# Masked attention on one core: context products in groups of four slot blocks, twelve exponentials' buffers, a new deal of the other work

## The chip, the cores and the metric

The kernel runs on one core of one Trainium2 chip. The metric is the time of one execution in device microseconds (us), lower is better. Before the change it is 1081.12 us, the median of three runs (1079.87 to 1084.78).

The engines of the core are named as in the profile: PE is TensorE (matrix products), with PEld for its weight loads, DVE is VectorE, ACT is ScalarE, POOL is GpSimd, and SP is SyncE, which here only issues DMA transfers.

## What is computed

Sixteen batches of self-attention over 1024 tokens with 512 features and 8 heads of 64, in which queries, keys and values are one and the same projection, and a mask of zeros and ones (about half of them ones) says which tokens take part:

```python
xt = jnp.transpose(x, (0, 2, 1))              # x: (16, 512, 1024)
q = xt @ Wq.T
qh = q.reshape(B, T, NH, dk).transpose(0, 2, 1, 3)
scores = scale * jnp.einsum('bhqd,bhkd->bhqk', qh, qh)
logits = (scores * cmask + (1.0 - cmask) * NEG) * rmask
attn = jax.nn.softmax(logits, axis=-1)
ctx = jnp.einsum('bhqk,bhkd->bhqd', attn, qh)
out = ctx.transpose(0, 2, 1, 3).reshape(B, T, D) @ Wo.T
x = x + jnp.transpose(out, (0, 2, 1))
```

A column outside the mask gets no weight. A row outside the mask has equal logits, so its result is the same for all such tokens of a batch: the mean of the values, projected.

## The kernel before

**Slots.** The kernel computes the full attention only for the tokens inside the mask. Their indices are found on the chip (`slots`, `hot`, `index`), their rows are gathered by indirect DMAs on POOL's queue (`gather`, L339) and lie in 544 slots: four blocks of 128 and a tail of 32. Results are scattered back by POOL (L811).

**Matmul precision.** Products of 32-bit numbers are made of 16-bit halves: `xt` transposes the rows (L424), ACT and DVE split them into a high and a low half (L384, L385); a query product (`query`, L447) is twelve matmuls for 128 features and half of the slots. ACT copies it from PSUM (L450) and DVE sets the slots beyond the batch's count to zero (L453). `qsplit` splits the query (L461 to L463), and four DMAs of SP's queue spread the halves over the partitions into the tile `xx` (L468 to L471). One `xx` serves one pair of heads.

**Scores and exponentials.** `scores(b, p, i)` makes the scores of one head p, one block i of 128 slots against all 544, with four matmuls (L620) into one of two PSUM tiles `pss`; ACT takes the exponential (L624) into an SBUF tile tagged `p`, of which there are nine. The tail slots of four heads go together: sixteen matmuls with 32 weight columns (L595), an exponential (L599), two DVE operations (L604, L605), and four DMAs (L611, L612) into `pt`.

**Context.** `attend(b, p, i, ps)` multiplies the values by the exponentials: for a pair of heads and a block, four matmuls of 64 weight columns with 32-bit numbers (L643), each two rows in the trace, adding to one PSUM tile `pav` (there is only one). The trace calls their tile 128\*64; the tile of scores, queries and projections is 128\*128, and that of the tail scores 128\*32. With i = 4 the tail is added (L647) and ACT copies the sum (L651). `recip_sums` (L666 to L674) and `recip_rows` (L680, L683, and DMAs L685, L688 into `rb`) give the rows' reciprocal sums, `norm` (L711 to L717) scales the context by them, and `project` (L727, twelve matmuls of 512 columns, then L732) makes the output.

**Values and peaks.** `value(b, e)` transposes `xx` by matmuls with a constant (L497), ACT copies the values (L500), and DVE sums their squares (L484, L485). From these come, for four heads at once, upper bounds that are subtracted before the exponential: `peaks` (L541, L543), `top` (a transpose on PE, L549, and a reduction on DVE, L551) and `bottom` (a matmul, L558, and small DVE operations from L560 on). `range_x` (L392) is a check of ranges on DVE.

**The order of the work.** `run` loops over the batches. A batch has 18 stages: for each of four pairs of heads the four blocks, and two stages of tail scores (after the second stage, and before the last pair). A stage of a block issues the scores of the pair's first head, then part of a work list `m`, then the scores of the second head, then, in some stages, a group of context products, and then another part of `m`. The list `m` holds what belongs to the batches around: the end of the batch before (reciprocals, `norm`, `project`), and for the next batch the transposes, queries, values and peaks. How much of `m` each stage issues is set by two numbers a stage in `share`.

Context products wait one stage or more: `todo` takes what a stage makes, a stage of block 0 or 2 hands it to `ready`, and a stage of block 1 or 3 issues `ready`, the last block first. So a group holds two blocks, and it comes two stages after the scores of its first block. All matmuls of a group after the first are tied to the first one (`behind`, with high priority), so that a group is not cut. Above this order stands a scheduler that fixes each engine's final order from the issue order, priorities and its own costs; `high_priority` raises what it surrounds. Each engine then takes its instructions in that order and waits at semaphores. The functions `later` and `issue` put the SP and POOL transfers into their queues one by one, stage by stage.

Of the kernel before, what the change touches and what calls it, by code (L numbers as in the profile page):

```python
# [10 lines left out]
F32 = mybir.dt.float32  # L11
# [8 lines left out]
P = 128  # L20
# [10 lines left out]
C = 544  # L31
# [18 lines left out]
class Fast:  # L50
# [531 lines left out]
    def scores(self, b, p, i):  # L582


        nc, s = self.nc, self.st[b]
        if "z" not in s:
            s["z"] = self.sb([P, H, 4], F32, "z", 2)
            s["zt"] = self.sb([P, 2], F32, "zt", 2)
        if i is None:
            pt = self.ps_s.tile([P, 2, 512], F32, tag="s", name="pss")  # L590
            for a in range(2):
                for g in range(2):
                    for r in range(HG):
                        xx, k = s["xx"][2 * p + r // 2], r % 2
                        self.beat = nc.tensor.matmul(pt[r * CT:(r + 1) * CT, g, :CH], lhsT=xx[:, 2 * k, 512:C],  # L595
                                                     rhs=xx[:, 2 * k + a, g * CH:(g + 1) * CH],
                                                     start=(a == 0), stop=(a == 1)).ins
            t = self.sb([P, C], F32, "p", 9)
            nc.scalar.activation(t.rearrange("p (g c) -> p g c", g=2), pt[:, :, :CH], AF.Exp,  # L599
                                 bias=s["nm"][p][:, HG:], scale=SCALE, accum_out=s["zt"][:, p:p + 1])  # L600

            hi = self.sb([P, C], F32R, "c", 4)
            lo = t.bitcast(F32R)
            nc.vector.tensor_copy(hi, t)  # L604
            nc.vector.tensor_tensor(lo, t, hi.bitcast(F32), ALU.subtract)  # L605

            def spread():
                s["pt"] = self.sb([P, 2, C], F32R, "pt")
                half = slice(0, DK), slice(DK, P)
                for k in range(2):  # L610
                    nc.sync.dma_start(out=s["pt"][half[k], k, :].bitcast(F32), in_=hi[half[k]].bitcast(F32))  # L611
                    nc.sync.dma_start(out=s["pt"][half[1 - k], k, :].bitcast(F32), in_=lo[half[k]].bitcast(F32))  # L612

            self.later(spread)
            return None
        xx, k = s["xx"][p // 2], p % 2
        pt = self.ps_s.tile([P, 2, 512], F32, tag="s", name="pss")
        for a in range(2):
            for g in range(2):
                self.beat = nc.tensor.matmul(pt[:, g, :CH], lhsT=xx[:, 2 * k, i * P:(i + 1) * P],  # L620
                                             rhs=xx[:, 2 * k + a, g * CH:(g + 1) * CH],
                                             start=(a == 0), stop=(a == 1)).ins
        t = self.sb([P, C], F32, "p", 9)
        self.exp = [nc.scalar.activation(t.rearrange("p (g c) -> p g c", g=2), pt[:, :, :CH], AF.Exp,  # L624
                                         bias=s["nm"][p // HG][:, p % HG:p % HG + 1], scale=SCALE,
                                         accum_out=s["z"][:, p, i:i + 1]).ins]
        return t

    def attend(self, b, p, i, ps):
        nc, s = self.nc, self.st[b]  # L630

        if i == 1:
            s["pav"] = self.ps_av.tile([P, 2, 512], F32, tag="av", name="pav")
        for g in range(2):
            for k in (1, 0) if i < 4 else range(2):
                cols = slice(g * CH, (g + 1) * CH)
                if i < 4:
                    with ExitStack() as st:
                        if self.group_first:

                            st.enter_context(self.behind(self.group_first))
                            st.enter_context(self.tc.high_priority(offset=HPO))
                        mm = nc.tensor.matmul(s["pav"][k * DK:(k + 1) * DK, g, :CH], lhsT=s["v"][p][:, i, k * DK:(k + 1) * DK],  # L643
                                              rhs=ps[k][:, cols], start=(i == 1), stop=False)
                    self.group_first = self.group_first or mm.ins
                else:
                    nc.tensor.matmul(s["pav"][:, g, :CH], lhsT=s["vt"][p // 2][:, k, p % 2 * 2:p % 2 * 2 + 2, :],  # L647
                                     rhs=s["pt"][:, p % 2, cols], start=False, stop=(k == 1))
        if i == 4:
            c = self.sb([P, C], F32, "c", 4)  # L650
            nc.scalar.copy(c.rearrange("p (g c) -> p g c", g=2), s["pav"][:, :, :CH])  # L651
            s["c"].append(c)
# [192 lines left out]
    def run(self, flag):  # L845
# [14 lines left out]
        def value(n, e):  # L860
            return [(0.45, L(self.value, n, e))]
# [83 lines left out]
        if True:  # L945
            for b in range(B + 1):
                o, n = b - 1, b + 1
                if b == B:
                    self.last(o, todo)
                    break  # L950
                free, sums, rows, third, tail, rest = {}, [], [], [], [], []
                if b:
# [12 lines left out]
                if n < B:  # L965
                    q, x, v = (lambda e, g: query(n, e, g)), xt(n)[2 if b == 0 else 0:], (lambda e: [(0.25, L(self.value, n, e))])
                    tc, tv = ((lambda g, f=f, c=c: [(c, L(f, n, g))]) for f, c in ((self.tail_copy, 0), (self.value_tail, 0.25)))
                    rng = [(0, L(self.range_x, n, c)) for c in range(DC)]
                    ahead = b + 2 < B
                    hot, index = ([(c, L(f, b + 2))] if ahead else [] for f, c in ((self.hot, 0), (self.index, 0.2)))  # L970
                    take = [(0, L(self.gather, b + 2, j)) for j in range(5)] if ahead else []
                    m = sums + x[:2] + (value(b, 3) if b else []) + pk(b, 1) + second + x[2:4] + rows + x[4:]
                    for g in new[0]:
                        m += [(0, L(self.active, *g))]
                    m += q(0, 0) + tp(b, 1) + (q(0, 1) if b else bt(b, 1) + q(0, 1))
                    for g in new[0]:
                        m += [(0.3, L(self.slots, *g))]
                    for g in new[1]:
                        m += [(0, L(self.facts_sums, *g))]
                    m += (bt(b, 1) if b else hot) + q(1, 0) + third + ([] if b else index) + q(1, 1) + ([] if b else take)  # L980
                    for g in new[1]:
                        m += [(0.1, L(self.facts_end, *g))]
                    m += rng[:2] + tc(0) + tail + v(0) + P_(0) + tv(0) + rest + v(1) + P_(1) + (hot if b else []) + rng[2:] + q(2, 0) + (index if b else [])
                    m += pk(n, 0) + q(2, 1) + tp(n, 0) + P_(2) + (take if b else []) + q(3, 0) + v(2) + bt(n, 0)
                    m += q(3, 1) + tc(1) + [(0, L(self.means, n))] + P_(3) + tv(1)
                    if b == 0:
                        k = next(k for k, (c, f) in enumerate(m) if f is index[0][1])
                        for c in range(DC):
                            m.insert(k + 1 + 3 * c, (0, L(self.split, "o", c)))
                else:  # L990

                    places = [("xi", 8), ("xa", 13)]
                    come = [[L(self.late, x, j, *places[k % 2]) for j in range(5, 9)] for k, x in enumerate(rests[b])]
                    leave = [[L(self.rest, x, j) for j in range(5, 9)] for x in rests[b]]
                    free[0] = [L(self.late, b, 4)] + come[0]
                    for c, l in zip(come[1:] + [[]], leave):
                        free[0] += c + l
                    m = second + sums + value(b, 3) + pk(b, 1) + rows + [(0.6, lambda: None)]
                    m += tp(b, 1) + [(0.6, lambda: None)] + bt(b, 1) + [(2.6, L(self.project_means, b))] + third + [(1.2, lambda: None)] + P_(0, 1, 2, 3)
# [13 lines left out]
                    for k in range(2 * DC):  # L1013
                        free.setdefault(1 + k // 3, []).append(L(self.sum_half, 1, k))

                share = [(1.2, 0) if i is None else ((0.95, 0.95), (0.9, 0), (0.45, 0.95), (0.9, 0))[i] for _, i in S]
                unit = sum(c for c, _ in m) / sum(map(sum, share))
                done, goal, pos = 0.0, 0.0, 0

# [8 lines left out]
                for st, (p, i) in enumerate(S):  # L1028
# [13 lines left out]
                    for _ in range(1 if b < B - 2 else -(-len(self.urgent + self.spare) // (N - st))):  # L1042
                        self.issue()

                    if i in (0, 2):
                        ready, todo = todo, []
                    elif i in (1, 3):
                        self.group_first = None
                        for f in ready[1::-1] + ready[2:]:
                            f()  # L1050
                        ready = []
                    fill(share[st][1])
# [157 lines left out]
```

## Time and profile before

| | |
|---|---|
| median of 3 runs | 1081.12 us |
| the profiled execution | 1081.4 us |
| its span, first to last instruction | 1079.7 us |
| mean granted clock of TensorE | 0.995 |
| PE busy | 1038.1 us, 96% of the span |
| DVE busy | 745.6 us, 69% |
| ACT busy | 681.6 us, 63% |
| POOL busy | 303.0 us, 28% |
| mean DMA rate | 168 GB/s |

The profile is one execution, recorded by the hardware. A group line names the source line (L624 is line 624 of the kernel), the engine, the operation, what it writes and reads with the shapes and types, and how often it ran; then the total busy time in us, the mean duration of one in ns, and the idle time of the engine just before such instructions, with what ended it. A line of the waits names the engine and the instruction that waited, what it waited for, and the total in us, the times, and the longest in us. A line of the timeline starts with the time in us from the start of the span and a duration in us; a bracket at its end gives the idle time before it and what ended it. TensorE's instructions overlap and their ends are modelled, so for it the distance from start to start is what tells the time taken. The granted clock is the share of TensorE's full clock that it was given.

### The profile page before, as it was taken

What the parts mean: (1) busy time and instruction counts of PE and PEld (TensorE: products, weight loads), DVE (VectorE), ACT (ScalarE), POOL (GpSimd) and SP (SyncE); (2) the same over time, 40 slices, a digit from 0 to 9 for tenths busy, and PEclk for the clock granted to TensorE, in tenths of its full rate; (3) what the DMA queues carried; (4) which work ended last, traced back from release to release, by engine and by line L of the source; (5) the groups of instructions that cost most, each with busy time, mean ns of one, the idle gap of its engine ahead of it and who ended that gap; (6) DMA issues with size and microseconds to landing.
All of it is one profiled execution on the core that took longest, in us unless ns stands there. A gap on an engine that the chain in (4) does not pass through costs nothing.

```text
span 1079.7 us, 23837 instructions
## 1 busy us (share of the span) xinstructions
PE 1038.1 (96%) x8626; PEld 690.9 (64%) x8626; DVE 745.6 (69%) x2376; ACT 681.6 (63%) x1722; POOL 303.0 (28%) x303
## 2 busy tenths in 40 slices
PE   6889999999999999999999999999999999999996
PEld 6566667666666666666666666667666665666553
DVE  6687768676675767766785776868667775666553
ACT  5777667666676766666576666666666565665550
POOL 3101022222202223222233323222232331335652
PEclk9999999999999999999999999999999999999999
DMA  6746465556655554656556566554755554565752
GB/s 205 211 126 177 133 175 154 174 150 190 174 141 158 171 173 145 198 176 169 177 147 197 154 186 193 152 171 135 229 176 173 177 149 127 149 182 166 222 175 84
DMA packets 78125, 181.39 MB, mean 168 GB/s; under 512 B 15008, under 2 KB 16800, under 8 KB 78000
## 3 DMA queue, kind: packets, MB, share of 16 engines
q1 hardware_dynamic: 56816, 111.62, 36.6%
q0 software_dynamic: 21184, 68.18, 20.8%
q8 instruction: 70, 1.15, 0.5%
q14 instruction: 55, 0.45, 0.1%
HBM read 92.34 MB, written 33.91 MB: 117 GB/s over the span
## 4 chain that ended last, share of the span: by engine, by line
PE 82%; DMA 7%; DVE 3%; ACT 2%; issue 2%; SPq 2%; POOL 0%; POOLq 0%; ACTq 0%; DVEq 0%
PE pav L643 21%; PE pss L620 19%; PE pm L727 15%; PE pm L447 14%; DMA xx<-hl 6%; PE pm L424 3%; PE pav L647 3%; PE pss L595 2%; PE pm L497 2%; PE pm L680 1%; ACT q L450 1%; SPq L470 1%; ACT p L624 1%; PE pm L520 1%; DMA rb<-rd 1%
## 5 line engine op out<-in xcount | busy, mean ns | idle before, releaser
L624 ACT ACTIVATE p<-pss,nm 128x544 f32<-128x544 f32 x512 | 365.5, 717 | 210.5 <-PE pss L620 203.6
L620 PE MATMUL pss<-xx 128*128 128x272 f16 x2048 | 317.6, 280 | 3.1 <-ACT p L624 2.7
L643 PE MATMUL pav<-p,v 128*64 128x272 f32 x2048 | 262.9, 399 | 0.0
L620 PEld LDWEIGHTS <-xx 128*128 128x128 f16 x2048 | 191.9, 100 | 73.2 <-issue 27.7
L643 PEld LDWEIGHTS pav<-p,v 128*64 128x64 f32 x2048 | 135.6, 136 | 94.3 <-issue 27.1
L811 POOL DMA_INDIRECT y_out<-xa,idx x68 | 70.2, 1032 | 288.6 <-issue 91.5
L447 PE MATMUL pm<-xh,wqh 128*128 128x274 f16 (+1 forms) x512 | 143.3, 280 | 3.3 <-DVE nm L560 1.9
L447 PE MATMUL pm<-xl,wqh 128*128 128x274 f16 (+1 forms) x512 | 142.9, 279 | 0.2 <-DVE xl L385 0.2
L447 PE MATMUL pm<-xh,wql 128*128 128x274 f16 (+1 forms) x512 | 143.0, 279 | 0.0
L339 POOL DMA_INDIRECT xa<-x_in,idx x68 | 69.5, 1023 | 167.1 <-PE pss L620 71.0
L447 PEld LDWEIGHTS <-wqh 128*128 128x128 f16 x1024 | 99.3, 98 | 25.9 <-issue 6.7
L811 POOL DMA_INDIRECT y_out<-xi,idx x60 | 74.0, 1233 | 137.7 <-DVE xi L798 38.3
L624 ACT ACTIVATION_READ_ACCUMULATOR p<-pss,nm 128x1 f32 x512 | 102.6, 200 | 0.0
L450 ACT ACTIVATE q<-pm 128x272 f32<-128x272 f32 (+1 forms) x128 | 50.8, 397 | 81.6 <-PE pm L447 81.6
L727 PE MATMUL pm<-woh,ch 128*128 128x512 f16 x240 | 91.8, 382 | 0.3 <-DVE tmp L523 0.3
L727 PE MATMUL pm<-wol,ch 128*128 128x512 f16 x240 | 91.7, 382 | 0.0
L727 PE MATMUL pm<-woh,cl 128*128 128x512 f16 x240 | 91.5, 381 | 0.0
L732 DVE SCALAR_TENSOR_TENSOR xa<-pm,xa 128x512 f32<-128x512 f32 x60 | 41.4, 690 | 72.4 <-PE pm L727 72.3
L339 POOL DMA_INDIRECT xi<-x_in,idx x60 | 61.3, 1021 | 106.1 <-PE pss L620 49.5
L727 PEld LDWEIGHTS <-ch 128*128 128x128 f16 x480 | 46.7, 98 | 45.6 <-issue 2.2
L369 ACT ACTIVATE xm<-xm 128x1024 f32<-128x1024 f32 (+1 forms) x62 | 62.5, 1009 | 2.3 <-DMA xm<-x_nat_in 2.3
L711 DVE TENSOR_TENSOR c<-c,rb 128x544 f32<-128x544 f32 x64 | 46.1, 720 | 22.4 <-PE pss L620 11.1
(194 smaller groups left out, 1550.0 us busy)
## 6 DMA issues: line engine op xcount, KB each, us to landing
xx<-hl SPq DMA_DIRECT2D x256, 136.0 KB
xm<-x_nat_in SPq DMA_DIRECT2D x56, 512.0 KB
rb<-rd SPq DMA_DIRECT2D x128, 136.0 KB
pt<-c SPq DMA_DIRECT2D x64, 136.0 KB
pt<-p SPq DMA_DIRECT2D x64, 136.0 KB
ub<-ud SPq DMA_DIRECT2D x16, 256.0 KB
xi<-x_nat_in SPq DMA_DIRECT2D x8, 256.0 KB
xa<-x_in,idx POOLq DMA_INDIRECT x68, 4.5
```

The costliest lines, as they stand in the source:

```text
L339: dma = self.nc.gpsimd.indirect_dma_start(out=tile[:n], out_offset=None, in_=self.x, in_offset=bass.IndirectOffsetOnAxis(ap=idx, axis=0))
L369: self.nc.scalar.activation(s["xm"][k], s["xm"][k], AF.Copy, accum_out=s["ms2"][:, k:k + 1])
L424: self.pe = nc.tensor.transpose(pt[:, c, :], x[:n, c * P:(c + 1) * P], self.ident[:n, :n]).ins
L447: self.beat = nc.tensor.matmul(pq, lhsT=w[:, c, e * P:(e + 1) * P], rhs=xx[:, c, cols], start=(k == 0), stop=(k == 3 * DC - 1)).ins
L450: nc.scalar.activation(s["q"][:, e, cols], pq, AF.Copy, scale=1.0 / (SX * SW))
L620: self.beat = nc.tensor.matmul(pt[:, g, :CH], lhsT=xx[:, 2 * k, i * P:(i + 1) * P], rhs=xx[:, 2 * k + a, g * CH:(g + 1) * CH], start=(a == ...
L624: self.exp = [nc.scalar.activation(t.rearrange("p (g c) -> p g c", g=2), pt[:, :, :CH], AF.Exp, bias=s["nm"][p // HG][:, p % HG:p % HG + 1 ...
L643: mm = nc.tensor.matmul(s["pav"][k * DK:(k + 1) * DK, g, :CH], lhsT=s["v"][p][:, i, k * DK:(k + 1) * DK], rhs=ps[k][:, cols], start=(i == ...
L711: self.once(nc.vector.tensor_tensor(c, c, s["rb"][p], ALU.mult), self.beat if p < 3 else None)
L727: nc.tensor.matmul(po[:cols.stop - cols.start], lhsT=a[:, e, cols], rhs=w[:, e, :], start=(e == 0 and k == 0), stop=(e == DC - 1 and k == 2))
L732: self.nc.vector.scalar_tensor_tensor(x, po, 1.0 / (SX * SW), x, ALU.mult, ALU.add)
L811: dma = self.nc.gpsimd.indirect_dma_start(out=self.out, out_offset=bass.IndirectOffsetOnAxis(ap=idx, axis=0), in_=x, in_offset=None)
```

## The change

Four things are edited.

- The tiles tagged `p`, which hold the exponentials until they are multiplied, become twelve instead of nine (L598 and L623).
- A group of context products holds the four blocks of a pair of heads. `ready` is taken over in the stage of block 0 only and issued in the stage of block 1 only, that is, in the second stage of the next pair, in the order 3, 2, 1, 0 and then the tail; the start flag of the accumulation moves from block 1 to block 3. `last` issues the blocks of the last pair in the same order.
- The work list `m` is put in another order. Value 3 of the batch goes after four transposes instead of two. The peaks of the batch's second four heads go to the end of the transposes, and their top goes behind the second query product. The values 0, 1 and 2 of the next batch move down: value 0 behind the first projection, value 1 behind the query product (2, 0), value 2 behind (3, 1); the peaks and the top of the first four heads go down with them.
- The numbers in `share` are new: more of `m` is issued in stages of block 2 and less in stages of block 1.

```diff
-            t = self.sb([P, C], F32, "p", 9)
+            t = self.sb([P, C], F32, "p", 12)
...
-        t = self.sb([P, C], F32, "p", 9)
+        t = self.sb([P, C], F32, "p", 12)
...
-        if i == 1:
+        if i == 3:
             s["pav"] = self.ps_av.tile([P, 2, 512], F32, tag="av", name="pav")
...
-                                              rhs=ps[k][:, cols], start=(i == 1), stop=False)
+                                              rhs=ps[k][:, cols], start=(i == 3), stop=False)
...
-                    self.last(o, todo)
+                    self.last(o, todo[3::-1] + todo[4:])
...
-                    m = sums + x[:2] + (value(b, 3) if b else []) + pk(b, 1) + second + x[2:4] + rows + x[4:]
+                    m = sums + x[:2] + second + x[2:4] + (value(b, 3) if b else []) + rows + x[4:] + pk(b, 1)
                     for g in new[0]:
                         m += [(0, L(self.active, *g))]
-                    m += q(0, 0) + tp(b, 1) + (q(0, 1) if b else bt(b, 1) + q(0, 1))
+                    m += q(0, 0) + (q(0, 1) + tp(b, 1) if b else tp(b, 1) + bt(b, 1) + q(0, 1))
...
-                    m += rng[:2] + tc(0) + tail + v(0) + P_(0) + tv(0) + rest + v(1) + P_(1) + (hot if b else []) + rng[2:] + q(2, 0) + (index if b else [])
-                    m += pk(n, 0) + q(2, 1) + tp(n, 0) + P_(2) + (take if b else []) + q(3, 0) + v(2) + bt(n, 0)
-                    m += q(3, 1) + tc(1) + [(0, L(self.means, n))] + P_(3) + tv(1)
+                    m += rng[:2] + tc(0) + tail + P_(0) + v(0) + tv(0) + rest + P_(1) + (hot if b else []) + rng[2:] + q(2, 0) + v(1) + (index if b else [])
+                    m += q(2, 1) + pk(n, 0) + P_(2) + (take if b else []) + tp(n, 0) + q(3, 0) + bt(n, 0)
+                    m += q(3, 1) + v(2) + tc(1) + [(0, L(self.means, n))] + P_(3) + tv(1)
...
-                share = [(1.2, 0) if i is None else ((0.95, 0.95), (0.9, 0), (0.45, 0.95), (0.9, 0))[i] for _, i in S]
+                share = [(1.2, 0) if i is None else ((1.0, 0.6), (0.1, 0.5), (0.9, 1.0), (0.9, 0.9))[i] for _, i in S]
...
-                    if i in (0, 2):
+                    if i == 0:
                         ready, todo = todo, []
-                    elif i in (1, 3):
+                    elif i == 1:
                         self.group_first = None
-                        for f in ready[1::-1] + ready[2:]:
+                        for f in ready[3::-1] + ready[4:]:
                             f()
                         ready = []
```

In the list, `q(e, g)` is a query product, `v(e)` a value of the next batch, `P_(i)` the projection of block i of the batch before, `x` the transposes of the next batch, `pk`, `tp` and `bt` the peaks, top and bottom, `tc` and `tv` the tail's copy and values, `rng` the checks of ranges, and `rows`, `sums`, `second` the reciprocals and the `norm` of the batch before.

## Prediction

> **What bounds the kernel now.** I read the page's busy shares first, then its groups, then TensorE's waits, then the timeline around single places.
>
> ```profile
> PE 1038.1 (96%) x8626; PEld 690.9 (64%) x8626; DVE 745.6 (69%) x2376; ACT 681.6 (63%) x1722; POOL 303.0 (28%) x303
> L624 ACT ACTIVATE p<-pss,nm 128x544 f32<-128x544 f32 x512 | 365.5, 717 | 210.5 <-PE pss L620 203.6
> ```
>
> TensorE is the bound: 1038.1 of 1079.7 us. ScalarE idles 203.6 us before its exponentials because TensorE has not written the scores, so anything gained must come off TensorE's stream: an instruction, a pause between instructions, or a wait. No matmul is removed. TensorE's waits:
>
> ```profile
> PE pm L497 <- DMA xx<-hl: 11.4, 15, 1.9
> PE pss L620 <- ACT p L624: 2.7, 4, 1.1
> PE pm L447 <- DVE nm L560: 1.9, 2, 1.4
> ```
>
> The value transposes (L497) wait 15 times, about once a batch, for the spread of the query they read. Hardly anything else waits. The pauses are seen only in TensorE's timeline; each row gives the start, the modelled duration and the count, so I subtract starts from starts. A stage with a context group, and one at the end where two groups have run together:
>
> ```profile
> 507.64 0.63 PE L620 MATMUL pss<-xx 128*128 128x272 f16 x4
> 508.20 2.06 PE L643 MATMUL pav<-p,v 128*64 128x272 f32 x16
> 510.18 0.33 PE L680 MATMUL pm<-ident,rcol 128*128 128x128 f32 x1
> ...
> 1050.88 1.09 PE L620 MATMUL pss<-xx 128*128 128x272 f16 x8
> 1051.81 0.18 PE L408 MATMUL pm<-okr,on 128*128 128x24 f16 x1
> 1051.91 2.97 PE L643 MATMUL pav<-p,v 128*64 128x272 f32 x24
> 1054.81 0.64 PE L620 MATMUL pss<-xx 128*128 128x272 f16 x4
> ```
>
> **Part 1: groups of four blocks.** Eight L620 take 1051.81 − 1050.88 = 0.93 us, so four take 0.46; before the group four take 508.20 − 507.64 = 0.56. Entering costs 0.10. Sixteen rows take 510.18 − 508.20 = 1.98, twenty-four 1054.81 − 1051.91 = 2.90: eight rows cost 0.92, so sixteen would cost 1.84, and 0.14 is paid once however long the group is. A group therefore costs 0.24 us beyond its matmuls. The order of the built kernel has 64 groups of 32 rows for 128 of 16. 64 × 0.24 = **−15.4 us**. The Trainium skill gives a reason and another price: "TensorEngine Tiling (Array Packing)", Key Properties, says that changing the tiling mode drains TensorE (L643 is 128*64, its neighbours 128*128), and "TensorE: Matmul & The Clock Gate", Single matmul latency, puts a drain at some 175 ns; two drains a group would be an estimated 350 ns, 64 × 0.35 = 22 us. I take the row.
>
> What the group needs hides it: its first block is now the one whose exponential came last, but the scheduler puts at least 1.6 us of other TensorE work between that score and the group. The twelve p buffers (nine before) hold eight waiting tiles, the tail tile and the next three; the order places the group ahead of the score that would need a thirteenth. Without that cover each group would wait one exponential, 0.72 us.
>
> **Part 2: tail scores in one piece.** The order shows L595 in 35 pieces instead of 62. In 14 batches the tail stage of heads 0 to 3 was cut as in the last six lines; the first two are an uncut one, of heads 4 to 7:
>
> ```profile
> 532.09 0.65 PE L595 MATMUL pss<-xx 128*32 128x272 f16 x16
> 532.67 0.64 PE L620 MATMUL pss<-xx 128*128 128x272 f16 x4
> ...
> 554.12 0.29 PE L595 MATMUL pss<-xx 128*32 128x272 f16 x1
> 554.34 0.33 PE L680 MATMUL pm<-ident,rcol 128*128 128x128 f32 x1
> 554.60 0.53 PE L595 MATMUL pss<-xx 128*32 128x272 f16 x12
> 555.06 0.43 PE L424 MATMUL pm<-ident,xt 32*128 32x32 f32 x4
> 555.42 0.30 PE L595 MATMUL pss<-xx 128*32 128x272 f16 x3
> 555.65 0.29 PE L620 MATMUL pss<-xx 128*128 128x272 f16 x1
> ```
>
> From 554.12 to 555.65 is 1.53 us. L680 costs 0.165 and four L424 of this size 0.32 by their usual spacing, leaving 1.05 for sixteen L595; in one piece they take 0.58. That is 0.47 × 14 = −6.6 us. But the uncut stage followed a context group directly in 14 batches and shared its switch; now it stands apart and pays its own entry, 0.10 × 14 = +1.4. Net **−5.1 us**.
>
> **Part 3: the values later.** Value e reads the xx that four DMAs on SP's queue fill (L468 to L471). The worst place:
>
> ```profile
> 891.39 0.19 PE L497 MATMUL pm<-two,xx 128*128 128x64 f16 x1 [1.91 <-DMA xx<-hl]
> ...
> 893.62 0.36 PE L497 MATMUL pm<-two,xx 128*128 128x64 f16 x7 [1.15 <-DMA xx<-hl]
> ```
>
> Between the query and value 0 TensorE has about 6.9 us of work in before, and is short by up to 1.91 + 1.15 = 3.1. In the new order a projection (twelve L727 of 0.216 = 2.6) and more stand between: 14.3 us of work by the same durations, and about 14 for values 1 to 3. Only batch 0 stays near its need: 6.6 us ahead of value 2 against about 7.5. Of the 11.4 some 10 go: **−10.0 us**. After those two waits the granted clock was 0.76 in the stretch 895 to 900, and the L727 start 0.43 apart, not 0.216, for 3.4 us; without the waits that is **−1.7 us**. SP's queue gets the same transfers in the same batch; what moves is which TensorE work surrounds them.
>
> **Part 4: what becomes late.** The list moves the peaks of group 1 (L541, L543) to after the last transpose, top (L549) behind two queries, bottom (L558) close behind top. In before, top at 557.28 and bottom at 559.27 have a score and a whole query between them, 2.0 us, and VectorE's reduction L551 is done with 0.5 to spare:
>
> ```profile
> 557.17 0.71 DVE L392 TENSOR_REDUCE top<-xh 128x1 f32<-128x545 f16 x1
> 557.80 0.72 DVE L605 TENSOR_TENSOR p<-p,c 128x544 fp32r<-128x544 f32 x1
> 558.43 0.28 DVE L551 TENSOR_REDUCE m<-pm 128x1 f32<-128x128 f32 x1
> ```
>
> In the new order bottom follows top after one score and at most one matmul in 12 of 15 batches: about 0.65 us of cover. VectorE's order puts one or two L392 (0.71), in most batches two L671 (0.15), and L453 (0.32), which itself needs ScalarE's copy of a query, between the peaks and L551. What TensorE waited for L551 in before was 0.4 us in two places; by that row the move costs nothing. Against the change speaks the skill's "Perfetto Trace Analysis", Tensor Engine Instruction (MATMUL, LD_WEIGHTS): VectorE and ScalarE take their queues strictly in order, so L551 can't pass an L392 even when top has long been written. By the rule, walking both engines from the copy of value 3, L551 ends some 1.6 us after top in eight batches and 1.3 in four, so 0.95 × 8 + 0.65 × 4 = 10 us. I take the rule, since the row had 2.0 us of cover. Bounds: 12 × 0 (L392 gets done early) to 12 × 1.7. Smaller: L680 late by 0.2 × 14 as VectorE reaches the reciprocals later; tail transposes waiting for the pm buffer that the value copy (0.585) frees, 0.3 × 8; 17 exponentials with less than 0.72 of TensorE work for cover, 0.15 each. These could be 7 together, but lie partly in the same idle time: I count 2. The sum is **+12 us** (bounds 0 and 27).
>
> **End.** The last group takes 16 more rows after the last exponential, 1.9 us, but the 24-row group before it goes, and the last projections cover the reciprocals' chain. I put **+1 us**, between −1 and +2.
>
> Sum against the profiled execution, 1081.4 us (span 1079.7, and 1.7 around it; 0.3 above the median of 1081.12): 1081.4 − 15.4 − 5.1 − 10.0 − 1.7 + 12 + 1 = **1062 us**.
>
> **The rivals.**
> (A) The sum above: own range 1055 to 1069.
> (B) The new VectorE waits stay hidden, since L392 waits for nothing and could run earlier: +1 in place of +12, 1051 us. For it: VectorE is busy 69%. Against: in the order L392 lies where it is counted.
> (C) They are twice as large, because each delays a query, its spread and then VectorE's next work: +24, 1074 us.
> (D) Slower: starvation after the long groups. During 3.8 us of context matmuls ScalarE has two scores to work on (1.4 us) and then idles 2.4, 64 times, where it idled 0.6 in each short one. Its 365.5 us of exponentials must then come faster between groups; where TensorE has less than 0.72 us of other work per score, it waits. One exponential a group would be 64 × 0.72 = 46: 1081.4 − 32.2 + 46 = 1095 us. The gains of 32.2 are used up from 0.50 us a group, and from 0.59 it is measurably slower. For it: the shares concentrate work in other stages. Against: TensorE waits for L624 only 2.7 us in before, and the new order leaves 0.57 us or more at every score.
> (E) The pause is not per group (the weight loads of a pair cause it): part 1 gives nothing, 1062 + 15.4 = 1077 us. Against: the 24-row group above paid once.
>
> **How the numbers follow.** A 0.50, B 0.20, C 0.16, D 0.08, E 0.06. About 0.5%, 5.4 us, is what a measurement of this kernel can tell. Faster (below 1075.7): A, B and two thirds of C, 0.81; within: E and most of the rest of C, 0.10; slower (above 1086.5): D and a little more, 0.09. The range of 8 in 10 leaves out D and the low edge of B: 1047 to 1080.
>
> **What would show it.** Right: L643 in 64 groups of 32 rows with start-to-start near 3.82 us (1.98 + 2 × 0.92) to the next instruction; L595 in single runs of 0.58; the wait of L497 for xx near 1 us; new waits of L558 for L551 of 0.6 to 1.0. Wrong: waits of L620 or L643 for L624 above 10 us in all, L643 for v or p, or a granted clock below 0.98 over the span.

## The result

The changed kernel takes 1063.74 us, the median of four runs (1062.39 to 1064.91), against 1081.39 us for the kernel before: a ratio of 0.9838, 95% interval 0.9818 to 0.9857. Run again later on another chip beside other kernels, it came to 0.9876 (0.9847 to 0.9905), a gain of 13.2 us for 17.7 here. The chips differ by 0.4% for the same kernel (the kernel before took 1085.6 us there), so below kernels are compared by their ratio to the kernel before on their own chip.

The page of the changed kernel, its busy shares and the group of the exponentials:

```profile
span 1063.1 us, 23765 instructions
PE 1021.6 (96%) x8626; PEld 701.6 (66%) x8626; DVE 729.2 (69%) x2376; ACT 672.5 (63%) x1722; POOL 298.6 (28%) x303
L624 ACT ACTIVATE p<-pss,nm 128x544 f32<-128x544 f32 x512 | 365.4, 718 | 217.5 <-PE pss L620 203.6
```

The same instructions ran, and TensorE is still busy for 96%: the span fell by 16.6 us and TensorE's busy time by 16.5. The time came out of TensorE's stream, as it had to. Its waits:

```profile
PE pm L680 <- DVE rcol L674: 6.3, 9, 0.7
PE pss L620 <- ACT p L624: 5.7, 13, 0.7
...
PE pm L447 <- DVE xa L732: 1.9, 5, 0.4
...
PE pm L558 <- DVE m L551: 1.1, 5, 0.2
```

The wait of L497 for the spread of the query is no longer listed. In its place stand L680, which waits for the reciprocals in nine batches, and L620. TensorE's timeline at a group, an uncut tail, and the two new waits (start, modelled duration):

```profile
485.17 0.65 PE L595 MATMUL pss<-xx 128*32 128x272 f16 x16
485.75 0.33 PE L680 MATMUL pm<-ident,rcol 128*128 128x128 f32 x1
...
490.78 0.27 PE L549 MATMUL pm<-ident,smcol 128*128 128x128 f32 x1
490.89 0.63 PE L620 MATMUL pss<-xx 128*128 128x272 f16 x4
492.00 0.28 PE L620 MATMUL pss<-xx 128*128 128x272 f16 x1 [0.48 <-ACT p L624]
492.11 0.36 PE L558 MATMUL pm<-ident,m 128*128 128x4 f32 x2
...
526.39 0.28 PE L558 MATMUL pm<-ident,m 128*128 128x4 f32 x2
527.38 0.30 PE L680 MATMUL pm<-ident,rcol 128*128 128x128 f32 x1 [0.70 <-DVE rcol L674]
527.51 0.63 PE L620 MATMUL pss<-xx 128*128 128x272 f16 x4
528.07 3.89 PE L643 MATMUL pav<-p,v 128*64 128x272 f32 x32
531.89 0.52 PE L620 MATMUL pss<-xx 128*128 128x272 f16 x3
```

A group takes 531.89 − 528.07 = 3.82 us, the figure that the prediction worked out.

Since a waiting matmul's modelled duration can hide a short wait, I also measured all traces in one other way. For each succession of two source lines on TensorE I took the usual distance from start to start (the lower twelfth over the kernels) and added up what goes beyond it by 25 ns or more, after the first 130 us, by the line that comes late:

| late on TensorE, us | all | L497 | L620 | L680 | L558 | L447 | L727 |
|---|---|---|---|---|---|---|---|
| before | 29.1 | 14.1 | 3.8 | 0 | 0 | 5.7 | 2.6 |
| changed | 34.8 | 0 | 13.0 | 8.7 | 1.8 | 5.2 | 1.5 |
| changed, again | 41.3 | 0 | 16.3 | 8.8 | 2.6 | 5.3 | 1.5 |
| groups alone | 54.7 | 18.7 | 21.4 | 1.6 | 1.1 | 2.4 | 5.4 |
| list and shares alone | 33.9 | 3.2 | 7.8 | 8.7 | 4.2 | 5.8 | 1.1 |
| values put back | 46.3 | 13.8 | 15.6 | 3.8 | 2.5 | 3.2 | 1.3 |
| groups cut in two | 43.6 | 0 | 16.1 | 7.7 | 5.0 | 7.1 | 1.4 |
| shares of before | 52.2 | 9.6 | 20.6 | 2.3 | 4.5 | 5.7 | 1.2 |
| one share set to 0 | 34.6 | 3.1 | 16.7 | 1.1 | 4.6 | 4.9 | 1.3 |
| nine buffers | 53.1 | 0 | 26.5 | 7.9 | 2.6 | 6.8 | 1.5 |
| rows later | 31.2 | 1.6 | 15.4 | 1.1 | 2.8 | 4.9 | 1.5 |
| rows and bottom later | 30.2 | 1.3 | 13.1 | 1.9 | 0.6 | 7.1 | 1.3 |

(0 stands for a line not among the nine largest, all below 1 us. The two kernels of the last section with the sums moved are not in the table.) A row is one execution, and some lie away from the median of their kernel: the groups alone took 1093.92 us in it (median 1088.55, the longest of ten), the values put back 1076.42 (1079.74, the shortest of ten).

The account of the change in its own trace, by starts, the tail scores and what comes late taken after the first 130 us: the context groups, 126 of 1.99 us and two odd ones before and 64 of 3.82 after, went from 254.7 to 244.4 us, and 64 entries of 0.094 fell away, −16.3; the tail scores with their entries went from 24.5 to 19.6, −4.9; what comes late rose from 29.1 to 34.8, +5.7. Together −15.5, of −16.6 in the span.

### The profile page after: what moved, and what is told of

Same layout as the page of the kernel before. It is cut to its first block, busy times and chain, and to the rows that moved or that the text cites. A ratio compares the mean times of both kernels' runs of the same rounds, so it can differ in the third digit from the quotient of the medians.

```text
span 1063.1 us, 23765 instructions
## 1 busy us (share of the span) xinstructions
PE 1021.6 (96%) x8626; PEld 701.6 (66%) x8626; DVE 729.2 (69%) x2376; ACT 672.5 (63%) x1722; POOL 298.6 (28%) x303
## 4 chain that ended last, share of the span: by engine, by line
PE 76%; ACT 10%; DVE 7%; issue 3%; DMA 2%; POOL 0%; POOLq 0%; DVEq 0%; SPq 0%; ACTq 0%
PE pav L643 22%; PE pss L620 17%; PE pm L727 15%; PE pm L447 12%; ACT p L624 5%; PE pm L424 2%; PE pav L647 2%; ACT xh L384 1%; DVE p L605 1%; ACT xm L369 1%; PE pss L595 1%; PE pm L497 1%; PE pm L680 1%; ACT v L500 1%; ACT p L599 1%
## 5 line engine op out<-in xcount | busy, mean ns | idle before, releaser
L624 ACT ACTIVATE p<-pss,nm 128x544 f32<-128x544 f32 x512 | 365.4, 718 | 217.5 <-PE pss L620 203.6
L620 PE MATMUL pss<-xx 128*128 128x272 f16 x2048 | 307.0, 280 | 6.5 <-ACT p L624 5.7
L643 PE MATMUL pav<-p,v 128*64 128x272 f32 x2048 | 248.8, 396 | 0.0
L620 PEld LDWEIGHTS <-xx 128*128 128x128 f16 x2048 | 194.7, 99 | 63.3 <-issue 22.5
L643 PEld LDWEIGHTS pav<-p,v 128*64 128x64 f32 x2048 | 141.4, 137 | 91.0 <-issue 13.9
L447 PE MATMUL pm<-xh,wqh 128*128 128x274 f16 (+1 forms) x512 | 143.9, 281 | 2.4 <-DVE xa L732 1.9
L447 PE MATMUL pm<-xh,wql 128*128 128x274 f16 (+1 forms) x512 | 143.2, 280 | 0.0
L447 PE MATMUL pm<-xl,wqh 128*128 128x274 f16 (+1 forms) x512 | 143.1, 280 | 0.0
L447 PEld LDWEIGHTS <-wqh 128*128 128x128 f16 x1024 | 98.1, 99 | 25.8 <-issue 4.8
L624 ACT ACTIVATION_READ_ACCUMULATOR p<-pss,nm 128x1 f32 x512 | 104.0, 203 | 0.0
L811 POOL DMA_INDIRECT y_out<-xi,idx x60 | 69.5, 1159 | 107.5 <-PE pss L620 49.0
L727 PE MATMUL pm<-woh,ch 128*128 128x512 f16 x240 | 91.1, 380 | 0.0
L727 PE MATMUL pm<-woh,cl 128*128 128x512 f16 x240 | 90.9, 379 | 0.0
L727 PE MATMUL pm<-wol,ch 128*128 128x512 f16 x240 | 90.9, 379 | 0.0
L732 DVE SCALAR_TENSOR_TENSOR xa<-pm,xa 128x512 f32<-128x512 f32 x60 | 41.3, 688 | 63.3 <-PE pm L727 59.9
L727 PEld LDWEIGHTS <-ch 128*128 128x128 f16 x480 | 45.6, 98 | 45.9 <-issue 1.4
L798 DVE TENSOR_TENSOR xi<-xi,ub 128x512 f32<-128x512 f32 (+1 forms) x60 | 40.9, 688 | 42.6 <-PE pss L620 42.0
```

Of the source, the lines that this page charges most:

```text
L447: self.beat = nc.tensor.matmul(pq, lhsT=w[:, c, e * P:(e + 1) * P], rhs=xx[:, c, cols], start=(k == 0), stop=(k == 3 * DC - 1)).ins
L727: nc.tensor.matmul(po[:cols.stop - cols.start], lhsT=a[:, e, cols], rhs=w[:, e, :], start=(e == 0 and k == 0), stop=(e == DC - 1 and k == 2))
L732: self.nc.vector.scalar_tensor_tensor(x, po, 1.0 / (SX * SW), x, ALU.mult, ALU.add)
L798: self.once(self.nc.vector.tensor_tensor(x[:n], x[:n], s["ub"][:n], ALU.add), self.beat)
L811: dma = self.nc.gpsimd.indirect_dma_start(out=self.out, out_offset=bass.IndirectOffsetOnAxis(ap=idx, axis=0), in_=x, in_offset=None)
```

## The experiments

### Which part brings the gain

Four kernels ran on one chip, the two of this section and the two of the next. The first has the groups of four and the twelve buffers, with `m` and `share` of before; the second has the new `m` and `share`, with groups of two and nine buffers.

```diff
-        t = self.sb([P, C], F32, "p", 9)
+        t = self.sb([P, C], F32, "p", 12)
...
-                    if i in (0, 2):
+                    if i == 0:
                         ready, todo = todo, []
-                    elif i in (1, 3):
+                    elif i == 1:
                         self.group_first = None
-                        for f in ready[1::-1] + ready[2:]:
+                        for f in ready[3::-1] + ready[4:]:
```

> The groups of four and the twelve buffers alone, with the list and the shares of before. Theory (the pause is paid per group and nothing else of the change is needed for it): 64 groups of 32 rows, 3.82 us each, -15.4 to -16.2 us; the values still wait for xx some 10 us as in before; the tail scores are still cut in about 14 batches: about 1065 us. Rival 1 (the pause is not per group): 1080 us. Rival 2 (the old shares starve ScalarE after a group of 3.8 us, one exponential of 0.72 us a group or more): the gain is used up, 1081 us or slower, with more than 20 us of L620 waiting for L624.

Measured: 1088.55 us against 1085.63, 1.0029 (1.0010 to 1.0048). Slower, where I had expected 1065.

The other has only the lines of `m` and `share`:

```diff
-                share = [(1.2, 0) if i is None else ((0.95, 0.95), (0.9, 0), (0.45, 0.95), (0.9, 0))[i] for _, i in S]
+                share = [(1.2, 0) if i is None else ((1.0, 0.6), (0.1, 0.5), (0.9, 1.0), (0.9, 0.9))[i] for _, i in S]
...
-                    m = sums + x[:2] + (value(b, 3) if b else []) + pk(b, 1) + second + x[2:4] + rows + x[4:]
+                    m = sums + x[:2] + second + x[2:4] + (value(b, 3) if b else []) + rows + x[4:] + pk(b, 1)
...
```

> The new list and the new shares alone, with groups of two blocks and nine buffers. Theory (sum of parts): L497 no longer waits for xx, -10, half-clock stretch gone, -1.7, tail scores in one piece in most batches, -3 to -5, and the new waits of the order come with it (L680 for the reciprocals, L447, L620), +7 to +12: 1070 to 1078 us. Rival (the list pays nothing, the new waits eat the values' gain): 1081 us. Rival (the list brings nearly all of the gain): 1066 us or less.

Measured: 1080.97 us, 0.9953 (0.9938 to 0.9969), 4.7 us faster by the medians, at the upper edge of what the sum had given.

The pause itself is saved in the first kernel in full: its 64 groups take 3.82 us each and 244.4 us together, as in the changed one. But 25.6 us more come late on TensorE than in before (54.7 for 29.1), and 5.7 in the first 130 us. Two lines of its waits, of TensorE and of ScalarE:

```profile
PE pm L497 <- DMA xx<-hl: 15.3, 11, 2.5
...
ACT v L500 <- PE pm L497: 93.1, 38, 3.2
```

The values wait longer than in before (18.7 for 14.1 by starts), and ScalarE stands 93.1 us before it can copy them (L500), 19.0 in before. L620 comes late by 21.4 us in 137 places, most by 0.1 to 0.25 us; that these scores wait for exponentials held up behind a waiting L500 is argued, not shown. The listed wait of L620 for L624 is only 3.8 us, below the 20 that rival 2 named, because the modelled durations cover the short ones. As this execution is 5.4 us above its median, the 25.6 are more than a usual execution has. The groups alone lose, then, and the list and shares alone gain 4.7, and both together gain 13 to 18. The parts don't add: the sum of the two alone is −2. How the 4.7 divide between list and shares, and what twelve buffers do with groups of two, was not run.

### The pause, and the place of the values

The next two start from the changed kernel. One cuts each group into two halves:

```diff
+                    if i == 1:
+                        self.group_first = None
+                        for f in ready[3:1:-1]:
+                            f()
+                        ready[2:4] = []
                     fill(share[st][0], st == N - 1)
...
-                        for f in ready[3::-1] + ready[4:]:
+                        for f in ready[1::-1] + ready[2:]:
```

> The changed kernel with each group of four cut into two of two, with scores and the like in between; list, shares and buffers as changed. Theory (0.24 us for each entry and exit, whatever the length): 64 more pauses, +15.4 to +16.2: 1079 to 1080 us. Rival 1 (the pause belongs to each pair of rows): 1064 us. Rival 2 (long groups starve ScalarE, and short ones give part of the pause back): +8 to +12, 1072 to 1076 us, with fewer waits of L620 for L624 than in the changed kernel.

Measured: 1088.31 us, 1.0022 (1.0006 to 1.0038), slower than the changed kernel by 0.0146 to 0.0184 of 1085.6, 16 to 20 us. Its timeline:

```profile
535.17 0.63 PE L620 MATMUL pss<-xx 128*128 128x272 f16 x4
535.73 2.06 PE L643 MATMUL pav<-p,v 128*64 128x272 f32 x16
537.72 0.64 PE L620 MATMUL pss<-xx 128*128 128x272 f16 x4
538.28 2.05 PE L643 MATMUL pav<-p,v 128*64 128x272 f32 x16
540.27 0.29 PE L447 MATMUL pm<-xh,wqh 128*128 128x274 f16 x1
```

Each half costs 1.99 us and its own entry (537.72 to 538.28 is 0.56 for 0.46 us of scores). 126 × 1.986 + 3.82 = 254.0 against 244.4, and 63 entries of 0.094 more: 15.5 us of the difference is the pause. The pause is per group, as the prediction had it; the rival that ties it to the rows is out, and so is the one that short groups give something back, since no less comes late here (43.6 us, for 34.8 and 41.3 in the changed kernel's two traces).

The other puts the values back to their places:

```diff
-                    m += rng[:2] + tc(0) + tail + P_(0) + v(0) + tv(0) + rest + P_(1) + (hot if b else []) + rng[2:] + q(2, 0) + v(1) + (index if b else [])
-                    m += q(2, 1) + pk(n, 0) + P_(2) + (take if b else []) + tp(n, 0) + q(3, 0) + bt(n, 0)
-                    m += q(3, 1) + v(2) + tc(1) + [(0, L(self.means, n))] + P_(3) + tv(1)
+                    m += rng[:2] + tc(0) + tail + v(0) + P_(0) + tv(0) + rest + (v(1) if b else []) + P_(1) + (hot if b else []) + rng[2:] + q(2, 0) + ([] if b else v(1)) + (index if b else [])
+                    m += q(2, 1) + pk(n, 0) + P_(2) + (take if b else []) + tp(n, 0) + q(3, 0) + (v(2) if b else []) + bt(n, 0)
+                    m += q(3, 1) + ([] if b else v(2)) + tc(1) + [(0, L(self.means, n))] + P_(3) + tv(1)
```

> The changed kernel with values 0, 1 and 2 put back to their places of before in the list (batch 0 left as changed). Theory (the later place takes away the wait for the spread): L497 waits for xx again, 9 to 14 us in all, and the time is 1072 to 1076 us. Rival (the spread is hidden anyway, since the new shares also change what lies before the values): no wait, 1063 to 1065 us.

Measured: 1079.74 us, 0.9950 (0.9931 to 0.9970), 8 to 12 us slower than the changed kernel. Its waits:

```profile
PE pm L497 <- DMA xx<-hl: 10.2, 15, 1.6
PE pss L620 <- ACT p L624: 8.3, 15, 3.1
...
PE pm L680 <- DVE rcol L674: 2.1, 4, 0.6
```

The old wait is back in 15 places, 13.8 us by starts. L680 comes late by 3.8 us for 8.8, so 5 us of them are won back there; that this is because TensorE now waits earlier is not shown.

### Shares and buffers

The changed kernel itself ran beside the next ones, to have them on one chip.

> The changed kernel again, as the measure for the others on the same chip. Both theories: 0.984 of the kernel before, some 17 us.

Measured: 1072.38 us, 0.9876 (0.9847 to 0.9905), 13.2 us below the kernel before, less than the 17 expected.

The shares of before in it:

```diff
-                share = [(1.2, 0) if i is None else ((1.0, 0.6), (0.1, 0.5), (0.9, 1.0), (0.9, 0.9))[i] for _, i in S]
+                share = [(1.2, 0) if i is None else ((0.95, 0.95), (0.9, 0), (0.45, 0.95), (0.9, 0))[i] for _, i in S]
```

> The changed kernel with the shares of before: groups of four, twelve buffers and the new list stay. Theory (the shares keep ScalarE fed around a group of 3.8 us): L620 waits again as in the run of the groups alone, some 8 us more than in the changed kernel in all, the tail scores are cut in 18 places more by 0.23 us, +4: 0.995 of the kernel before, 12 us slower than the changed kernel. Rival (the list alone does it, the shares hardly matter): within 3 us of the changed kernel.

Measured: 1088.05 us, 1.0023 (1.0002 to 1.0044), 15.7 us slower than the changed kernel beside it. Without the shares nothing is left of the gain, though the 64 long groups are there. L620 comes late by 4.3 us more, L497 by 9.6 and L272 by 3.7, L680 by 6.5 less, and the tail scores take about 24 us in place of 19.6.

One number of them alone, on a third chip with the three kernels after it:

```diff
-                share = [(1.2, 0) if i is None else ((1.0, 0.6), (0.1, 0.5), (0.9, 1.0), (0.9, 0.9))[i] for _, i in S]
+                share = [(1.2, 0) if i is None else ((1.0, 0.6), (0.1, 0.5), (0.9, 1.0), (0.9, 0))[i] for _, i in S]
```

> The changed kernel with one number of the shares changed: after the second score of block 3 no other work (0 for 0.9), as in the shares of before, so that the last score of a pair and the first of the next lie next to each other; the rest of the list spreads over the other places. Theory (in before a context group stood in that place and covered the exponentials; with one group a pair nothing does): L620 waits 6 us or more longer in all than in the changed kernel, which makes it 7 to 14 us slower, 0.992 to 1.000 of the kernel before. Rival (what costs with the old shares is work put into the stage of the group itself, not this place): within 3 us of the changed kernel.

Measured: 1072.18 us against 1087.48, 0.9875 (0.9833 to 0.9917), no difference from the changed kernel. The theory falls as it was put: the bare place between two pairs is not what the old shares cost. L620 came late by 16.7 us for 16.3, or for 13 if the one idle of ScalarE told of at the end is taken off: less than 6 either way. The time is the same for a mixed reason: the tail scores are cut in two again in 13 stages (about 23 us for 19.6), L497, L558 and L520 come later by 6 together, and L680's 8.8 are down to 1.1. Which of the eight numbers of the shares it is stays open.

And the buffers of before, for both tiles tagged `p`:

```diff
-            t = self.sb([P, C], F32, "p", 12)
+            t = self.sb([P, C], F32, "p", 9)
...
-        t = self.sb([P, C], F32, "p", 12)
+        t = self.sb([P, C], F32, "p", 9)
```

> The changed kernel with nine buffers for the exponentials instead of twelve. Theory of the prediction (without the three more, a group waits for an exponential): up to 0.72 us a group, 10 to 46 us slower than the changed kernel. Rival (the two exponentials that lack a buffer get one after the first eight rows of the group, 0.95 us in, and are done before its end at 3.8 us): 0 to 4 us slower.

Measured: 1087.60 us, 0.9999 (0.9976 to 1.0023): all of the gain is gone, some 13 us. ScalarE's waits, and then TensorE's, in this kernel:

```profile
ACT p L624 <- PE pss L620: 125.1, 96, 3.1
ACT p L624 <- PE pav L643: 61.5, 39, 3.9
...
ACT p L624 <- DMA pt<-p: 14.1, 9, 2.7
```

```profile
PE pss L620 <- ACT p L624: 16.8, 19, 3.0
```

With twelve buffers ScalarE waited 4.9 us for L643 and not at all for the tail's DMAs. With nine an exponential has no place to write to until the group frees one, or the four DMAs have read the tail tile, and TensorE's next score waits for it: L620 late by 26.5 us. My rival, that they are all done before the group ends, is out. The time lies at the low end of the theory's 10 to 46 us: 13 to 17 us over 64 groups is 0.2 to 0.27 us a group, not a whole exponential of 0.72.

### The new waits

The rows of pair 2 one stage later:

```diff
-                            free.setdefault(st + 3, []).append(L(self.recip_rows, b, p))
+                            free.setdefault(st + (4 if p == 2 else 3), []).append(L(self.recip_rows, b, p))
```

> The changed kernel with the reciprocals' rows of pair 2 (L680 and what follows) one stage later. Theory (L680 is late by 0.85 us in nine batches because VectorE has L604, L671, L605 and L671 to do after the tail's exponential, and everything on TensorE queues behind it): -6 to -8 us against the changed kernel, L680 no longer in the waits. Rival (TensorE's wait there hides other waits, above all of the next scores for their exponentials): -2 us or less, with L620 waiting more.

Measured: 1064.97 us, 0.9813 (0.9785 to 0.9842), 7.4 us below the changed kernel beside it. L680's late time fell from 8.8 to 1.1 us; L620's is 15.4 for 16.3, or for 13 without ScalarE's one idle, so at most some 2 us of it came back there. The wait was mostly L680's own. How much of the 7.4 us it is, the ratios leave open, since the changed kernel's on the first chip, 0.9838 (0.9818 to 0.9857), overlaps with this one. But from the first score of the third batch to the first of the last, which leaves out the start and the end, the profiled execution takes 819.7 us, for 825.2 and 826.4 in the changed kernel's two: 5.5 to 6.7 us are gained there.

What stood behind it is seen in VectorE's timeline of the changed kernel, from the tail's exponential to the last reciprocal:

```profile
524.90 0.48 DVE L604 CAST c<-p 128x544 fp32r<-128x544 f32 x1 [0.33 <-ACT p L599]
525.29 0.30 DVE L671 TENSOR_TENSOR rcol<-zt,corr 32x1 f32<-32x1 f32 x2
525.62 0.72 DVE L605 TENSOR_TENSOR p<-p,c 128x544 fp32r<-128x544 f32 x1
526.27 0.17 DVE L672 TENSOR_SCALAR rcol<-rcol 128x10 f32<-128x10 f32 x1
526.47 0.31 DVE L671 TENSOR_TENSOR rcol<-zt,corr 32x1 f32<-32x1 f32 x2
526.81 0.22 DVE L673 RECIPROCAL rcol<-rcol 128x10 f32<-128x10 f32 x1
527.06 0.17 DVE L674 TENSOR_TENSOR rcol<-rcol,hit 128x10 f32<-128x10 f32 x1
```

L671 needs the tail's sums, which ScalarE ended late; behind it stands L605 with 0.72 us for a tile that nothing on TensorE needs yet.

The sums moved into the groups' stages, in the changed kernel, with their loads:

```diff
-                        at = 3 * c + (0 if b else 4)
+                        at, to = ((0, 6), (3, 10), (7, 15), (11, 17))[c] if b else (3 * c + 4, 3 * c + 8)
                         free.setdefault(at, []).append(L(self.load_all, b + 2, c, None if b else first_top))
-                        free.setdefault(at + 4, []).append(L(self.sum_half, b + 2, c))
+                        free.setdefault(to, []).append(L(self.sum_half, b + 2, c))
```

> The changed kernel with the sums over the natural rows (L369, 1.05 us of ScalarE) moved into the stages with a context group, and their loads with them. Theory (nine waits of L620 of 0.64 us each come from an L369 ahead of the exponential): -4 to -6 us against the changed kernel. Rival (ScalarE is behind there anyway, the wait comes back at the next score or at another place): no change within 2 us.

Measured: 1071.28 us, 0.9870 (0.9836 to 0.9904), 1.1 us below: the rival. In the changed kernel L369 (1.04 us) does stand ahead of the late exponential in ScalarE's timeline:

```profile
489.82 1.04 ACT L369 ACTIVATE xm<-xm 128x1024 f32<-128x1024 f32 x1
490.77 0.19 ACT L369 ACTIVATION_READ_ACCUMULATOR xm<-xm 128x1 f32 x1
490.86 0.39 ACT L450 ACTIVATE q<-pm 128x274 f32<-128x274 f32 x1
491.14 0.71 ACT L624 ACTIVATE p<-pss,nm 128x544 f32<-128x544 f32 x1
```

The expectation's nine waits are six of 0.64 us at this place, between top (L549) and bottom (L558), and three of 0.6 us elsewhere near the end. With L369 gone from there, TensorE still waits at the same place:

```profile
492.43 0.63 PE L620 MATMUL pss<-xx 128*128 128x272 f16 x4
492.89 0.27 PE L549 MATMUL pm<-ident,smcol 128*128 128x128 f32 x1
493.00 0.63 PE L620 MATMUL pss<-xx 128*128 128x272 f16 x4
493.95 0.28 PE L620 MATMUL pss<-xx 128*128 128x272 f16 x1 [0.32 <-issue]
494.20 0.38 PE L558 MATMUL pm<-ident,m 128*128 128x4 f32 x2
```

From one score's end to the start of the next but one there are 0.57 us of other work, top and one score, and the exponential that has to free the PSUM tile takes 0.71. With L369 moved, this exponential starts 0.16 us sooner after top, and the third score is late by 0.48 us for 0.64. But the bottom then starts only 0.02 us sooner after top (1.31 for 1.33 us), as it is now late by 0.14 itself: it needs L551, which ends 1.25 us after top in both kernels, behind the L392 and the L453 that VectorE has ahead of it. In the changed kernel:

```profile
490.88 0.72 DVE L392 TENSOR_REDUCE top<-xh 128x1 f32<-128x545 f16 x1
491.52 0.32 DVE L453 TENSOR_TENSOR q<-q,hr 128x160 f32<-128x160 f32 x1
491.75 0.29 DVE L551 TENSOR_REDUCE m<-pm 128x1 f32<-128x128 f32 x1
```

It is so in all six places. Two waits end there within 0.1 us of each other, and where the first is shortened the second shows. The next kernel takes the bottom away from this place.

The bottom behind the query, beside the later rows:

```diff
-                    m += (bt(b, 1) if b else hot) + q(1, 0) + third + ([] if b else index) + q(1, 1) + ([] if b else take)
+                    m += ([] if b else hot) + q(1, 0) + (bt(b, 1) if b else []) + third + ([] if b else index) + q(1, 1) + ([] if b else take)
```

> The run with the rows of pair 2 one stage later, and besides the bottom of the second four heads (L558) behind the next query product instead of ahead of it. Theory (a bare pair of scores stands at top and bottom, so the next score waits for its exponential): the nine waits of L620 of 0.64 us and those of L558 go, -3 to -7 us against the run with the rows alone, 0.975 to 0.978 of the kernel before. Rival (ScalarE is late there whatever stands between, and the wait shows up at the next score): within 2 us of it.

Measured: 1061.63 us against 1087.48, 0.9771 (0.9726 to 0.9816). The waits of 0.64 us between L549 and L558 are gone, and L558's late time is 0.6 us for 2.8. Part of it comes back at the query products (L447), late by 7.1 us for 4.9, 0.30 in each of the six places; what comes late in all falls only from 31.2 to 30.2 us. From the third batch to the last it takes 817.2 us for 819.7 with the rows alone. Whether it beats that run can't be told: the intervals overlap.

The same with the edit of the sums from above:

> The same with the sums over the natural rows (L369) moved into the stages of the context groups as well. Theory (with the bare pair gone the 1.05 us of L369 are all that is left ahead of late exponentials): another -1 to -3 us. Rival (the wait was the pair's alone): no change within 1 us.

Measured: 1064.84 us, 0.9803 (0.9763 to 0.9843), on the same chip as the run before it and 3.2 us above it by the medians, though the intervals overlap. Moving L369 gains nothing here either; L447's wait for L732 doubles instead (4.2 us listed for 2.1), as it did in the first run with the sums moved (4.3). Rows and bottom later has the lowest median of this study, 25.9 us below the kernel before.

## Why the prediction was right, and where its steps were not

1062 us was predicted and 1063.74 measured; the sum held, and in the profile's own terms −19.2 was forecast for −16.6 measured. That it came so close is in part luck: two larger errors, 8 us too little for the new waits and 4 us too little for the values, went against each other. Part by part:

- **Groups, −15.4: held.** 3.82 us a group was the predicted figure, −16.3 with the entries' exact 0.094 each; cutting the groups gave 15.5 back. The estimate of 22 us from the two pages of the Trainium skill was too much: a group pays 0.25 us, 0.09 at its entry and 0.16 once inside or at its end (2 × 1.99 − 3.82), not 0.35.
- **Tail scores, −5.1: held,** −4.9.
- **Values, −10.0: right in kind, too small.** L497 came late by 14.1 us in before, more than the 11.4 that the waits list, so about 14 went. Put back, the values cost 8 to 12.
- **The half-clock stretch, −1.7: held.** In before eight L727 between 894 and 898 us come 0.21 late each; in the changed kernel the granted clock is full from 46 to 1056 us. L727 as a whole fell by only 1.1, since it now waits 0.57 for the last exponential.
- **New waits, +12: 20 by starts, and not made up as predicted.** What was to be 10 at L558 for L551 shows as 1.8. The wait is there, since VectorE gets to L551 late as the prediction's rule had it, but it is shorter than in the walk (L551 ends 1.25 us after top, not 1.6), and in six places it lies under another: the first matmul of the next score but one stands between top and bottom and waits 0.64 us for an exponential, until 1.22 us after top. Only in four places, where no such matmul stands there, does the bottom wait for L551, 0.38 each. I had costed L620 at 0.15 us in 17 places; it rose by 9.2. L680, taken as 2.8, is 8.7: nine times 0.85 and once 0.8. I saw its chain on VectorE and did not walk it from the tail's exponential. Together what is new is 8.7 + 9.2 + 1.8 = 20, against which I had counted 12, and the 4 that the values gave beyond my 10 made up half of that.
- **End, +1: mis-sized.** From the last score to the end of the span it is 27.7 us, 24.5 before: +3.2. Not 16 but 24 more rows of context stand behind the last score (32 for 8, 3.82 − 1.07 = 2.75 us); they are in the −16.3 already, and only the 0.57 of L727 comes on top.
- **What hides the group: the cover of twelve buffers** was priced at 0.72 us a group if gone; with nine it is 0.2 to 0.27.

Rival D, ScalarE starved around long groups, was given as a danger of the whole change. It did not come true for it, though its sign is less far off than the list of waits says: waits of L620 for L624 above 10 us were to show it, the list has 5.7, and by starts L620 is late by 13.0. And it names what the groups alone ran into: L620 late by 21.4 us and the values by 18.7. What the prediction got wrong in its form is that it costed the parts as if each paid by itself. The groups pay 16.3 only with the new shares and the buffers. With the old shares the gain goes into waits, most too short for the profile's list (10.9 us more comes late than in the changed kernel beside it), and into cut tail scores (about 4 more); with nine buffers it goes into TensorE's waits for exponentials that had no place to write to.

## What to carry to other kernels

Where an engine pays once for each change of tile shape, count the changes and take the price from a short and a long run in the same trace; that figure held to 6%. In this kernel a longer uninterrupted stretch on the bounding engine paid only when the engine that feeds it had buffers to run ahead into, and when the other work was dealt out anew around it; so plan these as one change and don't judge any of them alone. In walking a new order for waits, look at each score's distance to the one two before it as well as at the small reductions, and where two waits end together, expect little from removing one.

## What had not been expected

ScalarE idled before L779, near the end, in the changed kernel for 1.40 us in one execution and 4.09 in another, on another chip:

```profile
1002.40 0.59 ACT L779 ACTIVATE tmp<-pm 2x512 f32<-2x512 f32 x1 [4.09 <-issue]
```

The view names nothing that it waited for, but the trace's record of semaphore updates does: L779 waits for TensorE's signal that the last L727 is done. That L727 started at 999.24 us, and its signal is recorded at 1002.32, together with those of the two scores behind it (1002.38 and 1002.44); in the execution with 1.40 us it started at 996.42 and its signal came at 996.81. VectorE's next instruction started at 1002.47, and TensorE's next score waited 3.07 us for its exponential. The row stood between −0.1 and 4.1 us over the kernels of this study; it is part of why the changed kernel's two runs differ. In the execution with 4.09 the granted clock was then 0.52 from 1005 to 1010 us, and the last batch took 57.2 us from its first score to its last, for 51.4 in the other execution and 54.0 in the kernel with the rows later, which lacks the idle time. So some 3 us of the 7.4 that the later rows gained are this. With the sums moved, after an idle time of 4.05 us, it stayed at 1.00 from 1000 to 1010 us. Why the signals came so late stays open.
